# A selective scan on one core: the softplus through PSUM, all scaled tiles made by ScalarE, and its work placed at the head of a block

## The chip, the cores and the metric

The kernel runs on one NeuronCore of a Trainium2 chip, as one program in one launch. The metric is the time of an execution on the device, in microseconds. The engines are called as in the profile: PE is TensorE (PEld its weight loads), DVE is VectorE, ACT is ScalarE, POOL is GpSimd, SP is the queue that issues DMAs.

## The reference, cut to what matters

Eight samples of 256 channels on 32 x 32 positions go through four layers. The first three (attention with a gated feed-forward layer, a second attention, a quantised bottleneck) end in 8-bit codes in DRAM. The fourth is a state-space layer run in four directions over the 1024 positions, and all of the change but some prices lies there:

```python
def step(h, inp):
    u_t, dt_t, B_t, C_t = inp
    dA = jnp.exp(dt_t[:, :, None] * A)                      # A: 512 channels x 16 states
    h = h * dA + dt_t[:, :, None] * B_t[:, None, :] * u_t[:, :, None]
    y = jnp.einsum('bdn,bn->bd', h, C_t)
    return (h, y)
...
x = jax.nn.silu(xc).swapaxes(1, 2)
x_dbl = x @ W_x.T
dt = jax.nn.softplus(x_dbl[..., :DT_RANK] @ W_dt.T + b_dt)
...
y = _selective_scan(x, dt, A, Bm, Cm) + x * D
y = y * jax.nn.silu(z)
return y @ W_out.T
```

The four outputs (rows and columns, each forward and backward) are put back in place and added.

## The kernel before

The kernel has two phases. `phase_a` takes all samples through the first three layers; `phase_b` does the fourth.

Both are written as strands, Python generators that yield one operation or a list of them. `_Order.run` merges the strands into one program: it keeps its own clock for every engine, prices each operation in `_Op.__init__`, and always emits the operation that can start first by those clocks; at equal times the lower rank goes first. Each engine then executes its instructions in the order in which they were emitted, so the prices set the order of every queue but not the times on the chip. All operations are emitted in line 134, so the profile's groups are told apart by their tiles. Tiles come from rooms (`_Room`), each with a fixed number of buffers, and a strand that finds none waits.

In `phase_a` there is one thing more: where the order sees a gap on PE, `fill` puts in matmuls of constants (line 1077) that compute nothing needed, one for each 0.3 us of the gap.

`phase_b` works on blocks: 8 samples x 4 directions x 2 halves of 512 positions, 64 blocks, so that eight blocks make one sample. In a block there are 16 groups, one for each state s, and in each group four chunks c of 128 channels. The parts of a group are:

- `scales`: ACT multiplies duT (dt times x, positions on partitions; 128 x 512 for each of four position tiles t) with the column B of this state. The result is a tile of the room `dbu` (10 buffers). In every second group the last of the four position tiles is made another way: POOL multiplies the identity by B into a diagonal `dg`.
- `turns`: PE brings the four tiles of a chunk into a PSUM bank `db` (3 buffers) with channels on partitions. A scaled tile is transposed; for a diagonal, a full FP32 matmul of duT with the diagonal does the scaling and the turn at once.
- `decays`: ACT makes exp(dt * A) into `da` (5 buffers).
- `scans`: DVE runs the recurrence over 512 positions, from `da` and `db` into `h` (6 pairs). It frees `da` and `db`.
- `products`: POOL multiplies a pair of h by C, which a DMA spreads over the partitions (`cb`).
- `sums`: PE transposes the products and adds them up in four PSUM banks `py`.

Beside the groups there are jobs for blocks to come, started by `ahead` when the scans reach a given group: `mixed(n + 2)` (the convolution, the silu, B and C), `inputs` and `outputs` now and then, and `steps(n + 1)`, whose four dt jobs (one for each chunk) compute the softplus and duT, and entered at groups 0, 2, 4 and 6. These jobs rank ahead of all group work. They share one PSUM bank `pp`, taken with `lend()`.

A dt job computes the softplus as max(p, 0) + e - ((1 + e) - 1) + ln(1 + e), with e = exp(-|p|): ACT's Abs, Exp and Ln, DVE's `scalar_tensor_tensor` and `tensor_scalar`, and two POOL `tensor_tensor`. DVE then multiplies by x (tmp<-dt,xs), PE transposes the product (pp<-ident,tmp), and DVE copies it to duT (du<-pp).

Of the kernel before, what the change touches and what calls it, by code (L numbers as in the profile page):

```python
# [20 lines left out]
F32 = mybir.dt.float32  # L21
# [3 lines left out]
ALU = mybir.AluOpType  # L25
# [72 lines left out]
class _Op:  # L98


    def __init__(self, engine, method, args, kw):
        self.engine, self.method, self.args, self.kw = engine, method, args, kw
        out, ins = args[0], [a for a in (*args[1:], *kw.values()) if isinstance(a, bass.AP)]
        self.reads = {k for a in ins for k in self.blocks(a)}
        self.writes = {k for a in (out, kw.get("accum_out")) if a is not None for k in self.blocks(a)}
        self.landing = 0.0
        n = max(math.prod(a.shape[1:]) for a in (out, *ins)) / 1024
        near = all(a.space == out.space and out.space != PSUM for a in ins)
        if engine == "tensor":
            x = kw.get("rhs", ins[0])  # L110
            n = math.prod(x.shape[1:]) / 1024
            move = method == "transpose" or kw.get("is_transpose", False)
            self.cost = max(0.06, n * (0.93 if move else 0.44 if x.dtype != F32 else 1.76 if n > 0.2 else 2.1))
        elif engine == "vector":
            fast = near and method in ("tensor_scalar", "tensor_copy")
            both = near and method == "tensor_tensor"
            scan = method == "tensor_tensor_scan"
            self.cost = 0.04 + n * (2.2 if scan else 0.57 if fast else 1.1) + (0.3 if fast or both else 0)
        elif engine == "scalar":
            self.cost = 0.05 + 0.87 * n + (0.1 if len(ins) > 1 else 0)  # L120
        elif engine == "gpsimd":
            self.cost = 0.13 + 2.17 * n if method == "tensor_tensor" else 0.3 + n
        else:
            self.cost, self.landing = 0.1, 3.0

# [28 lines left out]
class _Room:  # L154
# [12 lines left out]
    def put(self, t):  # L167
        self.left.append(self.of.pop(t.name))


class _Order:
# [7 lines left out]
    def __init__(self, nc):  # L179
        self.nc, self.strands, self.n = nc, [], 0  # L180
        self.free, self.written, self.read, self.base, self.last = {}, {}, {}, {}, {}
        self.fill = None

    def add(self, rank, strand):
        self.n += 1
# [4 lines left out]
    def go(self, s, value=None):  # L190
        try:
            r = s[1].send(value)
            if isinstance(r, _Op):
                r = (r.cost, [r])
            elif isinstance(r, list):
                r = (sum(o.cost for o in r), r)
            s[2] = r
        except StopIteration:
            self.strands.remove(s)
# [63 lines left out]
def phase_a(ctx, tc, i, col, ident, codes, w_parts):  # L263
# [268 lines left out]
    def maxima(rank, q, k, rows, done):  # L532
# [6 lines left out]
        def some():  # L539
            while todo:  # L540
                yield lambda: not todo or may(2)
                if not todo:
                    break
                n = 4 if may(4) and not todo[0][2] else 2
                t, j, h = todo.pop(0)
                if n == 4 and todo:
                    todo.pop(0)
                bb = yield from some_banks(n)
                ops = []
                for e in range(n):  # L550
                    r = slice(32 * (h + e), 32 * (h + e) + 32)
                    ops.append(
                        T.matmul(bb[e], lhsT=q[r, t * P : (t + 1) * P], rhs=k[r, hs(j)], start=True, stop=True)
                    )
                yield (0.9 if n == 2 else 1.0, ops)
                for e in range(n):
                    m, s = (x[:, j, t, h + e : h + e + 1] for x in (least, sums))
                    yield V.tensor_reduce(m, bb[e], AX.X, ALU.max, negate=True)
                    yield A.activation(bb[e], bb[e], AF.Exp, bias=m, accum_out=s)
                    back(bb[e])  # L560
            left[0] -= 1
# [37 lines left out]
    def exponentials(rank, tasks, vt, n, finish):  # L599
# [5 lines left out]
        for task, (h, steps) in enumerate(tasks):  # L605
# [31 lines left out]
            def values(k, four, tiles, po=po, seen=seen, last=len(steps) - 1):  # L637
                es = [t[:, e] for t in tiles for e in range(2)]
                yield lambda: seen[0] == k
                ops = []  # L640
                for e, (q, kk, rows, key, r, c, at) in zip(es, four):
                    ops.append(
                        T.matmul(
                            po[at : at + n], lhsT=vt[:, key, c : c + n], rhs=e,
                            start=(k == 0 and key == 0), stop=(k == last), skip_group_check=True,
                        )
                    )
                yield (0.9 * (4 * n // P), ops)
                for t in tiles:
                    put(exps, t)  # L650
                seen[0] += 1
# [403 lines left out]
    def fill(gap, ops):  # L1055
# [6 lines left out]
            [order.last.get((bank.tag, k), 0.0) for k in bank.left] + [order.base.get(o.args[0].name, 0.0)] * own,  # L1062
            default=1e9,
        )
        n = int((gap - max(free, since)) / FILL)
        if n < 1:
            return
        if spare is not None and order.last.get((bank.tag, spare), 0.0) <= since:
# [9 lines left out]
        if t is not None:  # L1078
            bank.put(t)

    order.fill = fill
    stage = [0] * B

    def sample(b):
# [53 lines left out]
def phase_b(ctx, tc, i, col, ident, codes, w_parts, out):  # L1138
# [15 lines left out]
    xs_room = _Room(rooms, "xs", 11, [P, HALF])  # L1154
    dt_room = _Room(rooms, "dt", 2 * DC, [P, HALF])
    du_room = _Room(rooms, "du", 2, [P, TH, DI])
    db_room = _Room(rooms, "dbu", 10, [P, DI])
    dg_room = _Room(rooms, "dg", 4, [P, P])
    da_room = _Room(rooms, "da", 5, [P, HALF])
    h_room = _Room(rooms, "h", 6, [P, 2, HALF])  # L1160
    cb_room = _Room(rooms, "cb", 3, [P, HALF])
    tmp_room = _Room(rooms, "tmp", 3, [P, HALF])
    z_room = _Room(rooms, "z", 2, [P, HALF])
    cd_room = _Room(rooms, "cdb", 1, [P, CC, N], U8)
    wi_room = _Room(rooms, "wi", 2, [P, CC, 3, P], BF16)
# [29 lines left out]
    xds = [wp.tile([NX + 1, HALF], F32, name=f"xd{k}", tag=f"xd{k}") for k in range(2)]  # L1195
    for t in xds:
        nc.gpsimd.memset(t[2 * DS :], 1.0)
    zero = wp.tile([P, 1], F32, name="zero", tag="zero")
    nc.gpsimd.memset(zero, 0.0)
    yT = wp.tile([P, NT, DI], F32, name="yT", tag="yT")  # L1200
    ys = [wp.tile([P, N], F32, name=f"ys{c}", tag=f"ys{c}") for c in range(DC)]
    ctx.enter_context(tc.manual_schedule())
# [122 lines left out]
    def steps(n):  # L1325
# [6 lines left out]
        def dt(c):  # L1332
# [1 line left out]
            if c == 0:  # L1334
                d.duT[h] = yield from take(du_room)
            o = yield from take(dt_room)
            t, u1 = yield from takes(2, tmp_room)
            room, ps = yield from lend()
            yield T.matmul(ps, lhsT=w_dt[2 * DS :, c * P : (c + 1) * P], rhs=xd[2 * DS :], start=True, stop=True)
            left[0] -= 1  # L1340
# [4 lines left out]
            yield A.activation(t, ps, AF.Abs)  # L1345
            yield A.activation(t, t, AF.Exp, scale=-1.0)
            yield V.scalar_tensor_tensor(o, ps, 0.0, t, ALU.max, ALU.add)
            put(room, ps)
            yield V.tensor_scalar(u1, t, 1.0, -1.0, ALU.add, ALU.add)
            yield A.activation(t, t, AF.Ln, bias=1.0)  # L1350
            yield G.tensor_tensor(o, o, u1, ALU.subtract)
            yield G.tensor_tensor(o, o, t, ALU.add)
            put(tmp_room, t)
            d.dt[c, h] = o
            yield V.tensor_tensor(u1, o, d.xs[c, h], ALU.mult)
            yield lambda: h in d.duT
            room, pt = yield from lend()
            yield [T.transpose(pt[:, t * P : (t + 1) * P], u1[:, t * P : (t + 1) * P], ident) for t in range(TH)]
            put(tmp_room, u1)
            yield V.tensor_copy(d.duT[h][:, :, c * P : (c + 1) * P], pt.rearrange("p (t k) -> p t k", t=TH))  # L1360
            put(room, pt)
            done.add(("du", c))
# [76 lines left out]
    dbu, db, da, hh, cbs = {}, {}, {}, {}, {}  # L1439
    place = [0]  # L1440

    def scales(pick):


        for g, (n, d, h, s) in enumerate(groups):
            yield lambda: {("du", c) for c in range(DC)} | {"bT"} <= d.done[h]
            for t in range(TH):
                src, b = d.duT[h][:, t], d.bT[:, h * TH + t, s : s + 1]
                diagonal = t == TH - 1 and g % 2 == 0
                if diagonal != pick:  # L1450
                    continue
                if diagonal:
                    o = yield from take(dg_room)
                    yield G.tensor_scalar(o, ident, b, zero, ALU.mult, ALU.add)
                    dbu[g, t] = src, o
                else:
                    o = yield from take(db_room)
                    yield A.activation(o, src, AF.Identity, scale=b)
                    dbu[g, t] = o, ident

    def turns():
        for g, (n, d, h, s) in enumerate(groups):
            for c in range(DC):
# [1 line left out]
                ps = yield from take(ps_room)  # L1465
                yield [
                    T.matmul(
                        ps[:, t * P : (t + 1) * P], lhsT=dbu[g, t][0][:, c * P : (c + 1) * P], rhs=dbu[g, t][1],
                        is_transpose=dbu[g, t][1] is ident, start=True, stop=True,
                    )  # L1470
                    for t in range(TH)
                ]
                db[g, c] = ps
            for t in range(TH):
                o = dbu.pop((g, t))
                if o[1] is ident:
                    put(db_room, o[0])
                else:
                    put(dg_room, o[1])
            if s == DS - 1:  # L1480
                put(du_room, d.duT[h])

# [111 lines left out]
    def ahead():  # L1594

        for n in range(len(blocks)):
            jobs = []
            if n + 1 < len(blocks):
                jobs += zip((0, 2, 4, 6), steps(n + 1))
            if n + 2 < len(blocks):  # L1600
                jobs += zip((1, 3, 5, 7, 9, 10), mixed(n + 2))
            if n % 4 == 1 and n + 3 < len(blocks):
# [20 lines left out]
    for f in (list(inputs(0, False, xis[0, False])), mixed(0), steps(0), [behind(mixed(1))]):  # L1623
        for j in f:
            order.add((0, -1), j)
    for rank, f in enumerate((scans, decays, turns, lambda: scales(False), lambda: scales(True), products, sums, rows, ahead)):
        order.add((1, rank), f())
    order.add((0, -2), ends())
    order.run()
# [118 lines left out]
```

## Time and profile before

| | |
|---|---|
| median of three runs | 10703.6 us (10692.3 to 10710.2) |
| the profiled execution | 10710.8 us, span 10708.9 us |
| PE, DVE, ACT, POOL busy, share of the span | 92%, 79%, 81%, 63% |
| mean granted PE clock | 0.96 |
| 0 to 3747 us (to the first scan): PE, DVE, ACT, POOL busy | 3535, 2246, 2655, 911 us; clock 0.92 |
| 3747 to 10709 us: PE, DVE, ACT, POOL busy | 6364, 6241, 6047, 5826 us; clock 0.98 |

The profile is of one execution. The second phase repeats itself once per sample, which lets a view of one stretch stand for the others. Busy time of an instruction runs from its start to its end; instructions on PE and ACT overlap with those after them, so the distance between two starts in a row is shorter than a duration.

### The profile page before, as it was taken

The numbers are of one execution on the slowest core, as the hardware profiler recorded it, in microseconds if no ns is written. First come the engines' busy times: TensorE is split into PE (matmuls) and PEld (weight loads), VectorE is DVE, ScalarE is ACT, GpSimd is POOL, SyncE is SP. The second block draws the span as 40 slices with busy tenths as digits, with TensorE's granted clock in tenths as the row PEclk, the third lists the DMA queues.
The fourth block names the chain that finished last, engine by engine and source line by source line (L and its number), as shares of the span: only waits on it lengthen the run. The fifth ranks groups of instructions, "written<-read, shape, count | busy, mean of one in ns | idle before, by whom it ended". The sixth has DMA issues, their size and how long they took to land. (4 is left out here: it accounts for less than half of the span.)

```text
span 10708.9 us, 157325 instructions
## 1 busy us (share of the span) xinstructions
PE 9899.2 (92%) x58614; PEld 6251.0 (58%) x58726; DVE 8487.3 (79%) x8991; ACT 8702.0 (81%) x16284; POOL 6736.6 (63%) x3746
## 2 busy tenths in 40 slices
PE   9999999999999899899999999999989999998998
PEld 3333323333333267777777777777777777777776
DVE  5456657577675389888998998998899899899898
ACT  7867676777767488888888988888888888888988
POOL 1532133132220178888888888888888888888888
PEclk8998998999989899999999999999999999999999
DMA  1100000000000011111111111111111111111111
GB/s 53 32 18 16 22 17 22 13 22 13 14 13 10 20 46 41 48 52 47 47 46 52 50 42 56 41 49 52 45 48 52 47 47 46 51 50 43 56 40 50
DMA packets 217346, 410.01 MB, mean 38 GB/s; under 512 B 24881, under 2 KB 69297, under 8 KB 211458
## 3 DMA queue, kind: packets, MB, share of 16 engines
q1 hardware_dynamic: 216578, 399.94, 12.5%
q8 instruction: 461, 7.55, 0.3%
q14 instruction: 307, 2.51, 0.1%
HBM read 358.43 MB, written 30.93 MB: 36 GB/s over the span
## 5 line engine op out<-in xcount | busy, mean ns | idle before, releaser
L134 POOL TENSOR_TENSOR h<-h,cb 128x1024 f32<-128x1024 f32 x2048 | 4874.1, 2394 | 917.3 <-ACT st L134 462.7
L134 ACT ACTIVATE da<-dt,am 128x512 f32<-128x512 f32 x4096 | 2884.7, 717 | 515.6 <-DVE h L134 509.3
L134 DVE TENSOR_TENSOR_SCAN h<-da,st,db 128x512 f32<-128x512 f32 x2048 | 2469.2, 1260 | 177.2 <-PE db L134 96.9
L134 DVE TENSOR_TENSOR_SCAN h<-da,db 128x512 f32<-128x512 f32 x2048 | 2346.4, 1199 | 240.4 <-PE db L134 158.7
L134 ACT ACTIVATE dbu<-du,bT 128x512 f32<-128x512 f32 x3584 | 2487.7, 714 | 30.5 <-PE db L134 28.1
L134 PE MATMUL db<-ident,dbu 128*128 128x128 f32 x14336 | 2218.5, 280 | 169.1 <-DVE h L134 139.6
L134 PE MATMUL py<-ident,h 128*128 128x128 f32 x16384 | 2122.2, 275 | 91.5 <-POOL h L134 83.6
L134 PEld LDWEIGHTS db<-ident,dbu 128*128 128x128 f32 x14336 | 1669.9, 143 | 704.9 <-DVE h L134 377.9
L134 PEld LDWEIGHTS py<-ident,h 128*128 128x128 f32 x16384 | 1843.7, 142 | 168.4 <-POOL h L134 134.0
L134 DVE TENSOR_REDUCE stats<-bank 128x1 f32<-128x512 f32 x1536 | 983.0, 684 | 742.8 <-PE bank L134 741.3
L134 ACT ACTIVATE bank<-bank,stats 128x512 f32<-128x512 f32 x1536 | 1024.5, 672 | 380.9 <-DVE stats L134 370.4
L134 POOL TENSOR_TENSOR mid<-mid,mid 128x961 f32<-128x961 f32 (+2 forms) x192 | 400.3, 2092 | 1056.2 <-ACT mid L134 714.9
L134 PE MATMUL bank<-big,big 32*128 32x512 f32 x4096 | 913.3, 674 | 38.0 <-ACT bank L134 18.7
L134 PE MATMUL pp<-xi,cvd 128*128 128x512 f32 x2016 | 930.6, 605 | 3.5 <-DVE dt L134 1.5
L134 ACT ACTIVATE exps<-bank 128x512 f32<-128x512 f32 x1536 | 797.5, 620 | 135.6 <-PE bank L134 131.2
L134 PE MATMUL db<-dg,du 128*128 128x128 f32 x4096 | 809.0, 280 | 0.0
L134 DVE TENSOR_TENSOR tmp<-dt,xs 128x512 f32<-128x512 f32 x256 | 599.3, 2341 | 173.3 <-POOL dt L134 172.6
L134 POOL TENSOR_TENSOR dt<-dt,tmp 128x512 f32<-128x512 f32 x512 | 653.1, 1276 | 122.6 <-DVE tmp L134 97.5
L134 PEld LDWEIGHTS db<-dg,du 128*128 128x128 f32 x4096 | 636.2, 196 | 0.0
L134 DVE SCALAR_TENSOR_TENSOR mid<-mid,cols,mid 128x961 f32<-128x961 f32 (+1 forms) x384 | 597.2, 1555 | 6.9
L134 PEld LDWEIGHTS pp<-xi,cvd 128*128 128x128 f32 x2016 | 371.9, 195 | 384.3 <-issue 374.2
L134 PEld LDWEIGHTS bank<-big,big 32*128 32x128 f32 x4096 | 285.5, 193 | 503.2 <-issue 253.9
(212 smaller groups left out, 11329.5 us busy)
## 6 DMA issues: line engine op xcount, KB each, us to landing
cb<-c_d SPq DMA_DIRECT2D x1024, 256.0 KB, 3.2
wi<-w_in SPq DMA_DIRECT2D x192, 192.0 KB, 3.5
big<-in_x_dram SPq DMA_DIRECT2D x16, 1024.0 KB, 5.4
kept<-big SPq DMA_DIRECT2D x16, 1024.0 KB, 4.0
big<-kept SPq DMA_DIRECT2D x16, 1024.0 KB, 4.8
cdb<-codes SPq DMA_DIRECT2D x48, 256.0 KB, 4.2
big<-big SPq DMA_DIRECT2D x16, 512.0 KB, 6.7
out_dram<-z SPq DMA_DIRECT2D x32, 256.0 KB, 2.7
```

The source lines that it names most:

```text
L134: return getattr(getattr(nc, self.engine), self.method)(*self.args, **self.kw)
```

## The change

The edit has these parts:

- The softplus keeps its PSUM bank longer: (1 + e) - 1 is written over the bank instead of into a second SBUF tile, and DVE instead of POOL subtracts it. POOL instead of DVE multiplies dt by x, in place into the one tile t. The room `tmp` has 2 buffers, not 3, and a dt job takes one, not two.
- All four position tiles of every group are scaled by ACT and transposed; the diagonals, their room and their column of zeros are gone. The room `dbu` has 12 buffers, not 10.
- The dt jobs enter at groups 0, 1, 2 and 3.
- The ranks are reordered: decays and scales, which are ACT's, come after turns, products and sums.
- Prices of the order: matmuls over fewer than 20 rows cost 0.22 more, an ACT operation with a column operand 0.03 more, POOL's `tensor_tensor` 0.04 more. In `phase_a`, lists of PE operations get 0.1 more, three prices written by hand are set anew, and `fill` keeps 0.35 us of each gap.

```diff
-            self.cost = max(0.06, n * (0.93 if move else 0.44 if x.dtype != F32 else 1.76 if n > 0.2 else 2.1))
+            self.cost = max(0.06, (0.22 if x.shape[0] < 20 else 0) + n * (0.93 if move else 0.44 if x.dtype != F32 else 1.76 if n > 0.2 else 2.1))
...
-            self.cost = 0.05 + 0.87 * n + (0.1 if len(ins) > 1 else 0)
+            self.cost = 0.05 + 0.87 * n + (0.13 if len(ins) > 1 else 0)
         elif engine == "gpsimd":
-            self.cost = 0.13 + 2.17 * n if method == "tensor_tensor" else 0.3 + n
+            self.cost = 0.17 + 2.17 * n if method == "tensor_tensor" else 0.3 + n
...
-                r = (sum(o.cost for o in r), r)
+                r = (sum(o.cost for o in r) + self.way * (r[0].engine == "tensor"), r)
...
-                yield (0.9 if n == 2 else 1.0, ops)
+                yield (1.06, ops)
...
-                yield (0.9 * (4 * n // P), ops)
+                yield (0.88 * (4 * n // P) + 0.12, ops)
...
-        n = int((gap - max(free, since)) / FILL)
+        n = int((gap - max(free, since) - 0.35) / FILL)
...
-    order.fill = fill
+    order.fill, order.way = fill, 0.1
...
-    db_room = _Room(rooms, "dbu", 10, [P, DI])
-    dg_room = _Room(rooms, "dg", 4, [P, P])
+    db_room = _Room(rooms, "dbu", 12, [P, DI])
...
-    tmp_room = _Room(rooms, "tmp", 3, [P, HALF])
+    tmp_room = _Room(rooms, "tmp", 2, [P, HALF])
...
-            t, u1 = yield from takes(2, tmp_room)
+            t = yield from take(tmp_room)
...
             yield V.scalar_tensor_tensor(o, ps, 0.0, t, ALU.max, ALU.add)
+            yield V.tensor_scalar(ps, t, 1.0, -1.0, ALU.add, ALU.add)
+            yield A.activation(t, t, AF.Ln, bias=1.0)
+            yield V.tensor_tensor(o, o, ps, ALU.subtract)
             put(room, ps)
-            yield V.tensor_scalar(u1, t, 1.0, -1.0, ALU.add, ALU.add)
-            yield A.activation(t, t, AF.Ln, bias=1.0)
-            yield G.tensor_tensor(o, o, u1, ALU.subtract)
             yield G.tensor_tensor(o, o, t, ALU.add)
-            put(tmp_room, t)
             d.dt[c, h] = o
-            yield V.tensor_tensor(u1, o, d.xs[c, h], ALU.mult)
+            yield G.tensor_tensor(t, o, d.xs[c, h], ALU.mult)
...
-                diagonal = t == TH - 1 and g % 2 == 0
-                if diagonal != pick:
-                    continue
-                if diagonal:
-                    o = yield from take(dg_room)
-                    yield G.tensor_scalar(o, ident, b, zero, ALU.mult, ALU.add)
-                    dbu[g, t] = src, o
-                else:
-                    o = yield from take(db_room)
-                    yield A.activation(o, src, AF.Identity, scale=b)
-                    dbu[g, t] = o, ident
+                o = yield from take(db_room)
+                yield A.activation(o, src, AF.Identity, scale=b)
+                dbu[g, t] = o
...
-                        ps[:, t * P : (t + 1) * P], lhsT=dbu[g, t][0][:, c * P : (c + 1) * P], rhs=dbu[g, t][1],
-                        is_transpose=dbu[g, t][1] is ident, start=True, stop=True,
+                        ps[:, t * P : (t + 1) * P], lhsT=dbu[g, t][:, c * P : (c + 1) * P], rhs=ident,
+                        is_transpose=True, start=True, stop=True,
...
-                jobs += zip((0, 2, 4, 6), steps(n + 1))
+                jobs += zip((0, 1, 2, 3), steps(n + 1))
...
-    for rank, f in enumerate((scans, decays, turns, lambda: scales(False), lambda: scales(True), products, sums, rows, ahead)):
+    for rank, f in enumerate((scans, turns, products, sums, decays, scales, rows, ahead)):
```

More of the change, by code (lines that the diff above doesn't have):

```diff
@@ L181, in __init__ @@
         self.free, self.written, self.read, self.base, self.last = {}, {}, {}, {}, {}
-        self.fill = None
+        self.fill, self.way = None, 0.0
     def add(self, rank, strand):
@@ L1197, in phase_b @@
         nc.gpsimd.memset(t[2 * DS :], 1.0)
-    zero = wp.tile([P, 1], F32, name="zero", tag="zero")
-    nc.gpsimd.memset(zero, 0.0)
     yT = wp.tile([P, NT, DI], F32, name="yT", tag="yT")
@@ L1347, in dt @@
             yield V.scalar_tensor_tensor(o, ps, 0.0, t, ALU.max, ALU.add)
+            yield V.tensor_scalar(ps, t, 1.0, -1.0, ALU.add, ALU.add)
+            yield A.activation(t, t, AF.Ln, bias=1.0)
+            yield V.tensor_tensor(o, o, ps, ALU.subtract)
             put(room, ps)
-            yield V.tensor_scalar(u1, t, 1.0, -1.0, ALU.add, ALU.add)
-            yield A.activation(t, t, AF.Ln, bias=1.0)
-            yield G.tensor_tensor(o, o, u1, ALU.subtract)
             yield G.tensor_tensor(o, o, t, ALU.add)
-            put(tmp_room, t)
             d.dt[c, h] = o
-            yield V.tensor_tensor(u1, o, d.xs[c, h], ALU.mult)
+            yield G.tensor_tensor(t, o, d.xs[c, h], ALU.mult)
             yield lambda: h in d.duT
             room, pt = yield from lend()
-            yield [T.transpose(pt[:, t * P : (t + 1) * P], u1[:, t * P : (t + 1) * P], ident) for t in range(TH)]
-            put(tmp_room, u1)
+            yield [T.transpose(pt[:, k * P : (k + 1) * P], t[:, k * P : (k + 1) * P], ident) for k in range(TH)]
+            put(tmp_room, t)
             yield V.tensor_copy(d.duT[h][:, :, c * P : (c + 1) * P], pt.rearrange("p (t k) -> p t k", t=TH))
@@ L1440, in phase_b, with scales @@
     place = [0]
-    def scales(pick):
+    def scales():
         for g, (n, d, h, s) in enumerate(groups):
@@ L1474, in turns @@
             for t in range(TH):
[L1475 to L1479, printed above, removed]
+                put(db_room, dbu.pop((g, t)))
             if s == DS - 1:
```

## The prediction

> **What bounds the kernel now.** I read the busy time by stretches first. The scans start at 3747 us and fill the rest of the span; from 4077 us on the kernel repeats itself once per sample (eight blocks), so I cut the span at seven samples.
>
> ```profile
> core 0: us, PE busy (x) PEld busy (x) DVE busy (x) ACT busy (x) POOL busy (x), PEclk, DMA share, GB/s
> 6691.70:7563.30 871.60, 799.22 (x5379) 623.80 (x5394) 783.43 (x714) 759.31 (x1322) 729.57 (x409) 0.98 0.17 48
> ...
> sum 6094.00, PE 5587.71 PEld 4363.68 DVE 5480.19 ACT 5312.78 POOL 5108.57; mean PE 798.24 PEld 623.38 DVE 782.88 ACT 758.97 POOL 729.80
> ```
>
> A sample takes 6094/7 = 870.6 us, in which PE is busy 798, DVE 783, ACT 759, POOL 730. Nothing is saturated: four engines lie within 8% of each other, each with 70 to 140 us of waiting. So the second question is what they wait for (the waits of all engines from 4000 to 10500 us, 6500 us, or 7.47 samples):
>
> ```profile
> ACT da L134 <- DVE h L134: 480.8, 451, 5.7
> PE pp L134 <- DVE tmp L134: 188.2, 141, 2.1
> DVE tmp L134 <- POOL dt L134: 166.3, 106, 3.0
> ACT st L134 <- DVE h L134: 136.7, 172, 2.5
> ACT tmp L134 <- DVE tmp L134: 65.2, 86, 1.5
> ```
>
> Columns are us in total, times, longest. ACT's main wait is for one of the five da tiles, which a DVE scan frees: DVE is late. PE and DVE also wait for each other around tmp, the softplus. The third view is the groups with shapes kept apart, same window:
>
> ```profile
> L134 POOL TENSOR_TENSOR h<-h,cb 128x1024 f32<-128x1024 f32 x1918 | 4566.2, 2394 | 866.3 <-ACT st L134 428.7 <-DVE h L134 260.1 <-issue 53.5
> L134 ACT ACTIVATE da<-dt,am 128x512 f32<-128x512 f32 x3835 | 2700.4, 717 | 483.9 <-DVE h L134 480.8
> L134 ACT ACTIVATE dbu<-du,bT 128x512 f32<-128x512 f32 x3355 | 2328.6, 714 | 29.1 <-PE db L134 27.9
> ...
> L134 PE MATMUL db<-dg,du 128*128 128x128 f32 x3836 | 758.2, 280 | 0.0
> ...
> L134 DVE TENSOR_TENSOR tmp<-dt,xs 128x512 f32<-128x512 f32 x239 | 569.2, 2382 | 167.1 <-POOL dt L134 166.3
> ...
> L134 DVE TENSOR_SCALAR tmp<-tmp 128x512 f32<-128x512 f32 x239 | 271.2, 1135 | 0.0
> ...
> L134 POOL TENSOR_SCALAR dg<-ident,bT,zero 128x128 f32<-128x128 f32 x479 | 243.6, 509 | 69.8 <-PE db L134 69.0
> ```
>
> Two DVE steps cost more than their size: a 512-column multiply takes 2382 ns. The view of the tile tmp (min/median/max) shows why that is not its own work:
>
> ```profile
> L134 DVE TENSOR_SCALAR tmp<-tmp x239: 409/694/2589, 4004.1 to 10486.5; 128x512 f32<-128x512 f32 x120
> L134 DVE TENSOR_TENSOR tmp<-dt,xs x239: 666/2601/2852, 4009.8 to 10490.4; 128x512 f32<-128x512 f32 x120
> ```
>
> Alone the multiply takes 666 ns; mostly it takes two microseconds more, about one POOL h product (2394 ns).
>
> **What the skill says.** "SBUF — State Buffer", section "Who interferes with whom": a DVE instruction with two SBUF inputs, or in a two-port mode such as tensor_scalar from SBUF to SBUF, contends with GpSimd for a shared port, and the loser blocks for the whole instruction; with at most one SBUF input outside those modes it doesn't. The two rows agree. "TensorE: Matmul & The Clock Gate", section "Terms", calls transpose mode 4x faster for FP32; here it is 2x: in the PE instructions in order of time a diagonal product is two passes 0.11 us apart, a transpose one such pass. "ScalarE: Activation LUTs", section "What ACT_TABLE_LOAD costs", says that back-to-back ACTIVATEs overlap by about 93 ns; starts of dbu in a row lie 614 ns apart against 714 ns long, so I price them at 0.614 us.
>
> **The change, per sample** (32 dt jobs, 128 groups).
> - **DVE.** The multiply leaves: 32 x 2.38 = -76. tensor_scalar now writes PSUM, out of the two-port mode: 1.135 becomes about 0.67, the row of dt<-pp,tmp (667 ns): -15. The subtract comes in with one PSUM input; the three DVE steps now run in a row, starts 0.58 apart: +19. DVE 783 - 72 = 711. Bound: the contention stays with the tensor_scalar (2.5 us at most, +45) or all costs fall to 0.58 (-5); I take the table row.
> - **POOL.** 64 diagonals at 0.509 leave: -33. The subtract (1.275) is exchanged for the multiply, same shape and engine: 0. POOL 730 - 33 = 697.
> - **PE.** 64 x 4 diagonal products lose one pass: 256 x 0.11 = -28. The transposes of the softplus waited 188.2/7.47 = 25 us for the DVE multiply; now they wait for POOL. If a product comes in between, that is 32 x 2.34 = 75 us; if POOL's two steps follow at once, nothing. The order's own price of a POOL tensor_tensor (0.17 + 2.17/2 = 1.26 us) fits the measured 1.275, whereas it gave the DVE multiply 0.89 against 2.38, so PE's queue was placed 1.5 us too early; I take 10. Behind that wait stand turns and sums. PE 770.
> - **ACT.** 64 scaled tiles come in: 64 x 0.614 = +39. ACT 759 + 39 = **798**, now the busiest, at just what PE has today.
> - **Lent bank.** A dt job holds pp, the one spare PSUM bank, 4.2 us today (first matmul to the end of scalar_tensor_tensor); two more DVE steps make it 5.4: 32 x 1.2 = +38 us of pp. Folds, convs and projections queue behind it, with deadlines of a block or more. Taken as nothing; at worst +38.
> - **Order.** dt jobs enter at groups 0 to 3 of a block, not 0, 2, 4, 6. In those four groups POOL has 8 x 2.33 + 8 x 1.23 = 28.5 us and ACT some 28, against 27 of a quarter block: a lag of under 2 us, within the h tiles (three groups) and the twelve dbu. The results are needed a block later. The ranks keep decays before scales on ACT and turns before sums on PE, so they only break ties: 0. DMAs and the SP queue are unchanged.
>
> **From work to time.** ACT's period is its busy time plus its idle time, now 870.6 - 759 = 112. By the waits (divided by 7.47): da 64, st 18, tmp<-tmp 9, pp results 12, dbu 4, rest 5. The da wait arises when DVE frees no da tile, above all in a dt job: 0.67 + 1.135 + 2.38 + 0.70 of waiting = 4.9 us each, 156 per sample; after, some 1.8 us, 58. In proportion 64 becomes 24, and as ACT gets 39 us slower against DVE I take 12. st 13, tmp 6, pp results 12, rest 3: **46**. Period 798 + 46 = 844, -26 per sample, x 8 = **-210 us**.
>
> **The first phase** (to 3747 us) has the same code but other prices in its order: higher PE costs and 0.35 us kept back in every gap before filler matmuls are put in.
>
> ```profile
> L1077 PE MATMUL bank<-minus x1622: 376/379/634, 1.6 to 3657.7; 128*128 128x512 bf16 x175, 128*64 128x512 bf16 x6
> ```
>
> Counting in PE's order of time, the 1622 fillers stand in 445 runs, starts 0.215 us apart; after 359 of the runs the next matmul starts at once, so the run may have made it late. One filler less per run is 445 x 0.215 = 96 us of PE queue; I count **-40**, as DVE is only 60% and ACT 71% busy here and the chain is often theirs. Bounds: -110, and +60 if a lower clock (0.92 here) or the new order costs more.
>
> Sum against the profiled execution (span 10708.9, 10710.8 us in all, 7 above the median 10703.6): 10710.8 - 250 = 10461, or 10455 on the scale of the median.
>
> **Rivals.**
> 1. *ACT closes up (slower).* The scaled tiles go to what becomes the busiest engine and its waits stay, because the bunched dt jobs in the first four groups still stop scans and da tiles. Break-even is an ACT idle of 870.6 - 798 = 72 per sample (without the first phase). At 85 it costs 13 x 8 = 102, less 40: 10710.8 + 62 - 7 = 10766. For it: in before no engine passes 92%, and ACT would have to run at 94.6%. Against: 64 of its 112 idle us hang on a DVE that loses 72. Chance 0.13.
> 2. *Half of it (small or no gain).* The transposes wait for POOL (75) or the pp bank (38) eats what DVE gives: idle 65, -7 x 8 - 20 = -76, 10628. Chance 0.12, a third of it within the noise.
> 3. *More.* With prices that fit, ACT hardly stalls (idle 22, 97%): 820, -50 x 8 - 60 = -460, 10244. DVE scans do run back to back in quiet groups now. Chance 0.13.
>
> The forecast has 0.62, by itself from 10320 to 10630. The range over all cases is 10250 to 10720. A measurement of this kernel can tell 0.2% (21 us) from no change: faster 0.62 + 0.13 + 0.08 = 0.83, same 0.04, slower 0.13.
>
> **What would show it.** A sample near 844 us with ACT about 798 busy and above PE; DVE about 711, POOL about 697; no tmp<-dt,xs on DVE and no DVE row of the softplus over 0.7 us; da<-DVE h falling from 481 to some 90 in a like window; PE's wait for tmp now on POOL and under 75; fewer than 1250 fillers. It would be wrong if ACT's idle stayed over 72 per sample, if PE stayed the busiest, or if the first phase moved by more than 100.

## The result, and the profile after

The changed kernel takes 10311.6 us (median of four runs, 10309.9 to 10314.2) against 10706.9 for the kernel before, measured again beside it: a ratio of 0.9635, 95% interval 0.962 to 0.9651. The forecast was 10455 in a range of 10250 to 10720: right in sign, inside the range, but 143 us too slow. The profiled execution took 10309.9 us (span 10308.2), 401 less than the one before.

The first view is again the busy time by stretches, cut at the first scan and at seven samples.

```profile
core 0: us, PE busy (x) PEld busy (x) DVE busy (x) ACT busy (x) POOL busy (x), PEclk, DMA share, GB/s
0.00:3698.40 3698.40, 3447.14 (x15022) 1295.69 (x15023) 2255.81 (x3326) 2643.96 (x5756) 889.73 (x491) 0.90 0.06 21
3698.40:10308.20 6609.80, 6152.72 (x40960) 4742.00 (x40958) 5724.99 (x5671) 6304.93 (x11035) 5523.44 (x2736) 0.97 0.17 50
```

```profile
6478.40:7304.80 826.40, 771.68 (x5137) 593.75 (x5136) 717.68 (x714) 791.03 (x1385) 691.91 (x345) 0.97 0.17 51
...
sum 5779.50, PE 5407.34 PEld 4162.84 DVE 5022.64 ACT 5539.83 POOL 4842.20; mean PE 772.48 PEld 594.69 DVE 717.52 ACT 791.40 POOL 691.74
```

Of the 401 us, 49 lie in the first phase and 352 in the second. A sample takes 5779.5/7 = 825.6 us, not 870.6. ACT has become the busiest, at 791, and it now stands still for only 34 us of a sample, where it stood still for 112. The waits of ACT, over these seven samples (5779.5 us; in total, times, longest), show which of its stops went:

```profile
ACT da L134 <- DVE h L134: 154.5, 279, 1.9
ACT st L134 <- DVE h L134: 25.7, 69, 0.4
ACT xs L134 <- PE pp L134: 12.9, 42, 1.0
ACT tmp L134 <- PE pp L134: 12.9, 25, 1.1
ACT dbu L134 <- PE db L134: 10.4, 25, 1.4
ACT tmp L134 <- DVE pp L134: 2.3, 7, 0.3
```

The view of the tile tmp and of pp (min/median/max) shows the softplus on its new engines. No DVE row is stretched any more; compare 409/694/2589 and 666/2601/2852 before.

```profile
L134 DVE TENSOR_SCALAR pp<-tmp x238: 694/695/697, 4006.2 to 10096.7; 128x512 f32<-128x512 f32 x119
...
L134 POOL TENSOR_TENSOR tmp<-dt,xs x237: 1264/1277/1292, 4010.6 to 10092.8; 128x512 f32<-128x512 f32 x119
```

```profile
L134 DVE TENSOR_TENSOR dt<-dt,pp x238: 659/661/667, 4008.0 to 10098.4; 128x512 f32<-128x512 f32 x119
```

DVE's own idle time has grown, from 88 us to 108 per sample: in this window its scans wait 467.5 us for db, the bank that PE fills. That does not make it free time, as e_multdve below shows.

### The profile page after: what moved, and what is told of

Its sections match the earlier page's. It is cut to its first block, busy times and chain, and to the rows that moved or that the text cites. A ratio compares the mean times of both kernels' runs of the same rounds, so it can differ in the third digit from the quotient of the medians.

```text
span 10308.2 us, 152318 instructions
## 1 busy us (share of the span) xinstructions
PE 9599.9 (93%) x55980; PEld 6037.7 (59%) x55980; DVE 7980.8 (77%) x8997; ACT 8948.9 (87%) x16790; POOL 6413.2 (62%) x3227
## 3 DMA queue, kind: packets, MB, share of 16 engines
q1 hardware_dynamic: 216578, 399.94, 12.9%
## 4 chain that ended last, share of the span: by engine, by line
PE 38%; ACT 33%; DVE 21%; issue 5%; POOL 2%; DMA 1%; SPq 0%; DVEq 0%; POOLq 0%; ACTq 0%
PE bank L134 20%; ACT da L134 12%; ACT dbu L134 11%; DVE h L134 8%; PE pp L134 7%; PE py L134 5%; DVE mid L134 5%; PE db L134 5%; DVE stats L134 3%; ACT xs L134 2%; DVE dt L134 2%; ACT tmp L134 2%; PE bank L1077 1%; ACT z L134 1%; ACT bank L134 1%
## 5 line engine op out<-in xcount | busy, mean ns | idle before, releaser
L134 POOL TENSOR_TENSOR h<-h,cb 128x1024 f32<-128x1024 f32 x2048 | 4815.7, 2373 | 898.5 <-ACT st L134 322.4
L134 ACT ACTIVATE dbu<-du,bT 128x512 f32<-128x512 f32 x4096 | 2806.8, 709 | 12.5 <-PE db L134 10.6
L134 PE MATMUL db<-ident,dbu 128*128 128x128 f32 x16384 | 2411.4, 283 | 300.0 <-DVE h L134 208.2
L134 PEld LDWEIGHTS db<-ident,dbu 128*128 128x128 f32 x16384 | 1909.5, 144 | 870.4 <-DVE h L134 388.3
L134 PE MATMUL bank<-big,big 32*128 32x512 f32 x4096 | 958.9, 685 | 40.8 <-ACT bank L134 29.9
L134 PEld LDWEIGHTS bank<-big,big 32*128 32x128 f32 x4096 | 331.1, 197 | 523.9 <-issue 206.1
L134 POOL TENSOR_SCALAR big<-big,ga,gs 128x512 f32<-128x512 f32 x64 | 59.8, 948 | 818.6 <-DVE gs L134 480.5
L134 PE MATMUL bank<-exps,big 128*32 128x512 f32 (+1 forms) x3072 | 552.0, 627 | 3.7 <-ACT exps L134 3.7
L134 PE MATMUL bank<-big 32*128 32x512 f32 x2048 | 509.5, 724 | 21.3 <-ACT bank L134 17.9
L134 POOL TENSOR_TENSOR big<-big,mid 128x961 f32<-128x961 f32 (+1 forms) x128 | 315.1, 2470 | 227.0 <-ACT mid L134 224.4
```

What stands on the lines that cost most here:

```text
L134: return getattr(getattr(nc, self.engine), self.method)(*self.args, **self.kw)
```

## The experiments

I had two questions: which part carries the 352 us of the second phase, and why they were more than the 210 of the forecast. Each kernel was timed in three rounds against the kernel before. All samples below are blocks 3 to 58 of the profiled execution, divided by seven; ACT idle is the sample's time less ACT's busy time.

| kernel | time, us | ratio to before, 95% | first scan | sample | ACT busy | ACT idle |
|---|---|---|---|---|---|---|
| before | 10706.9 | | 3747 | 870.6 | 759 | 112 |
| after | 10311.6 | 0.9635 (0.962 to 0.9651) | 3698 | 825.6 | 791 | 34 |
| a_softplus | 10524.3 | 0.9827 (0.9811 to 0.9844) | 3745 | 848.5 | 758 | 91 |
| b_nodiag | 10718.8 | 1.0015 (1.0008 to 1.0022) | 3745 | 871.8 | 794 | 78 |
| c_first | 10659.3 | 0.9953 (0.9938 to 0.9968) | 3706 | 870.2 | 758 | 112 |
| h_place_alone | 10684.2 | 0.998 (0.9973 to 0.9987) | 3758 | 867.3 | 758 | 109 |
| f_price | 10822.0 | 1.0111 (1.0094 to 1.0128) | 3933 | 860.5 | 760 | 101 |
| e_multdve | 10543.1 | 0.9848 (0.9828 to 0.9868) | 3716 | 855.4 | 794 | 61 |
| k_diag | 10393.6 | 0.9713 (0.9695 to 0.9732) | 3692 | 836.9 | 757 | 80 |
| d_place | 10407.9 | 0.972 (0.9705 to 0.9734) | 3703 | 838.9 | 791 | 48 |
| m_apart | 10421.2 | 0.9732 (0.9717 to 0.9746) | 3708 | 839.7 | 794 | 46 |
| i_prices | 10394.1 | 0.9704 (0.9688 to 0.972) | 3717 | 836.1 | 793 | 43 |
| j_ranks | 10456.5 | 0.9766 (0.9743 to 0.9789) | 3702 | 843.3 | 793 | 51 |
| g_conv | 10294.2 | 0.9614 (0.9599 to 0.9628) | 3695 | 824.7 | 775 | 50 |

### One part alone, on the kernel before

**a_softplus.** The new softplus only:

```diff
-            t, u1 = yield from takes(2, tmp_room)
+            t = yield from take(tmp_room)
...
+            yield V.tensor_scalar(ps, t, 1.0, -1.0, ALU.add, ALU.add)
+            yield A.activation(t, t, AF.Ln, bias=1.0)
+            yield V.tensor_tensor(o, o, ps, ALU.subtract)
...
+            yield G.tensor_tensor(t, o, d.xs[c, h], ALU.mult)
```

> The kernel before with the softplus part alone: (1+e)-1 into the PSUM bank, the subtract on DVE, the multiply on POOL, two tmp tiles; diagonals, order of the dt jobs and all prices as before. Theory T (DVE's contention with POOL was what starved ACT of da tiles): most of the gain of the second phase is here, a sample falls from 871 to about 840 us, -240 us in all (ratio 0.978), the da<-DVE h wait halves at least. Rival D (what counts is PE's and POOL's relief from the diagonals): -60 us (0.994).

Measured: 183 us faster, all of it in the second phase (6776.7 us from the first scan on, before 6961.6). ACT's work is unchanged and its idle time falls by 21 us per sample. Its da wait falls from 447.3 us in seven samples to 254.1. So theory T is right on the direction and high on the size: 183, not 240, and the da wait falls by 43%, not by the half that it asked for. The run does not part two things: DVE loses no time to POOL any more, and the order's price of the multiply now fits (f_price takes up the second). Another wait grew in the same view:

```profile
ACT da L134 <- DVE h L134: 254.1, 377, 2.5
ACT xs L134 <- PE pp L134: 238.3, 114, 6.0
```

ACT's wait for the convs of pp was 59.3 and is 238.3. A dt job now holds the lent bank for 6.9 us in the kernel after (from its first matmul to the end of the subtract, mean of 252 jobs in the list of instructions) and 6.6 here, against 4.2 before.

**b_nodiag.** All tiles scaled by ACT, no diagonals:

```diff
-                diagonal = t == TH - 1 and g % 2 == 0
-                if diagonal != pick:
-                    continue
...
+                o = yield from take(db_room)
+                yield A.activation(o, src, AF.Identity, scale=b)
```

> The kernel before with all four tiles of a group scaled by ACT and transposed, no diagonals, eleven dbu tiles (twelve do not fit beside three tmp tiles); softplus, order and prices as before. Theory T: ACT gets 39 us of work per sample more, DVE stays late, so a sample goes from 871 to 875 or 890 us, +30 to +150 us (ratio 1.003 to 1.014). Rival D: PE and POOL lose 28 and 33 us per sample and that carries the gain: -200 us or more (0.981).

Measured: 11 us slower, just clear of zero. ACT's work grows by 35 us per sample and its idle time shrinks by 34. Rival D falls: with the old softplus, relief of PE and POOL is worth what it costs ACT and no more.

**c_first.** The first phase's edits alone, from `yield (1.06, ops)` to `order.fill, order.way = fill, 0.1` of the diff.

> The kernel before with the first phase's edits alone: the three prices written by hand, 0.1 us per list of PE operations, 0.35 us kept back in each gap before fillers. Both theories: the second phase stays within 5 us; the first falls by about 50 us (ratio 0.995), with some 950 fillers for 1622. If the change of the first phase came from the shared prices of operations instead, less than 15 us.

Measured: 48 us faster, the first scan 42 us earlier, a sample 870.2. Fewer fillers and the new prices came together here, so the run does not say which of the two paid. The fillers, in the view of line 1077:

```profile
L1077 PE MATMUL bank<-minus x946: 376/379/634, 1.6 to 3614.6; 128*128 128x512 bf16 x177, 128*64 128x512 bf16 x13
```

**h_place_alone.** `zip((0, 1, 2, 3), steps(n + 1))` in the kernel before.

> The kernel before with the dt jobs at groups 0, 1, 2, 3 and nothing else: here a dt job gives its pp bank back right after scalar_tensor_tensor. Theory B (the place pays because the softplus now holds the one lent bank longer, and convs no longer have to share the groups with it): little or nothing, within 30 us of before (ratio 0.997 to 1.003). Rival O (bunching at the head pays by itself): some 90 us faster (0.992 or less).

Measured: 21 us faster, as theory B had it, though its interval just excludes 1. In the profiled execution the second phase is 30 us shorter and the first, with the same instructions as before, 11 us longer: so much can a first scan differ by itself. The place was worth more at the other end of the change, as d_place shows.

**f_price.** Only what the order believes of DVE:

```diff
-            self.cost = 0.04 + n * (2.2 if scan else 0.57 if fast else 1.1) + (0.3 if fast or both else 0)
+            self.cost = 0.04 + n * (2.2 if scan else 0.57 if fast else 1.1) + (0.8 if fast else 1.8 if both else 0)
```

> The kernel before with one price changed: the order counts DVE's SBUF-to-SBUF tensor_tensor at 2.4 us and tensor_scalar at 1.1 us in the two phases, as measured; nothing else. Theory T: the time itself is lost on DVE and stays lost, so at most 40 us faster (ratio 0.996 or more). Rival P (the order was wrong because its price was wrong): PE no longer waits 25 us per sample for tmp, 100 us or more faster (0.990 or less).

Measured: 117 us slower, and neither theory meant that. The price also holds in the first phase, where the order then sees longer gaps and fills them: 2586 fillers for 1622, and the first scan comes 186 us later. The second phase went the other way, from 6961.6 to 6892.8, 69 us faster. So rival P has a share: some of what the multiply cost was that the order did not know its time. PE's wait for tmp did not vanish by it (PE pp <- DVE tmp is still 96.4 us in seven samples).

### One part taken back, from the kernel after

**e_multdve.** `yield V.tensor_tensor(t, o, d.xs[c, h], ALU.mult)` in place of POOL's.

> The kernel after with the multiply of dt by x put back on DVE (two SBUF inputs), at the order's old price of 0.89 us. Theory T (DVE's wait for POOL's port holds the scans and so the da tiles): the DVE row of the multiply is 2 us or more again, ACT's da wait grows from 154 to 300 us or more in a like window, 100 us or more slower than the kernel after (ratio to before 0.973 or more). Rival S (DVE has slack now, 108 us per sample idle): 66 us of contention per sample is absorbed, within 30 us of the kernel after (0.966 or less).

Measured: 232 us slower. Rival S falls, although DVE was idle for 108 us of a sample. The groups of DVE show a stretched multiply again, though at 1.6 us and not the 2 or more that T expected; min/median/max from the tile's view stand below it:

```profile
L134 DVE TENSOR_TENSOR tmp<-dt,xs 128x512 f32<-128x512 f32 x224 | 354.7, 1583 | 1.1 <-POOL dt L134 0.9
```

```profile
L134 DVE TENSOR_TENSOR tmp<-dt,xs x228: 665/1507/2837, 4044.0 to 10079.7; 128x512 f32<-128x512 f32 x114
```

The shortest is 665 ns, the mean 1583, which agrees with the shared port of the Trainium skill's page "SBUF — State Buffer", section "Who interferes with whom". DVE gets 32 x 1.58 = 51 us of work per sample, 29 of them contention; the sample grows by 30, ACT's idle time by 27. The da wait is 220.9, not the 300 that T expected; ACT's wait for st (103.9 for 25.7) and PE's for dbu (113.2 for 56.6) grew as well.

**k_diag.** The diagonals back in, with ten dbu tiles and four dg tiles.

> The kernel after with the diagonals back (every second group, one position tile of four; ten dbu tiles and four dg), the new softplus, order and prices kept. Theory T: ACT loses 32 us of work per sample and PE gets 28, POOL 33; PE becomes the busiest at some 800 and the sample takes 835 us, 80 us slower than the kernel after (ratio 0.971). Rival A (ACT is the bound, so taking work from it pays): 100 us faster than the kernel after (0.954).

Measured: 82 us slower, as theory T had it. With the new softplus the extra ACT work is worth having, with the old one (b_nodiag) it was not. PE is the busiest again, at 791 us of a sample to ACT's 757, and the da wait more than doubles:

```profile
ACT da L134 <- DVE h L134: 351.1, 493, 3.3
```

**d_place.** The dt jobs back at groups 0, 2, 4, 6.

> The kernel after with the dt jobs back at groups 0, 2, 4, 6. Theory T: no one waits for dt within the block, so within 0.3% of the kernel after (10280 to 10340 us, ratio to before 0.960 to 0.966). Rival O (the place in the block matters): slower than the kernel after by 100 us or more (ratio 0.973 or above).

Measured: 96 us slower, just short of the 100 of rival O and far from theory T: my prediction, which gave the order 0, is wrong on this. ACT's waits pointed to the lent bank:

```profile
ACT da L134 <- DVE h L134: 182.4, 258, 3.2
ACT xs L134 <- PE pp L134: 80.3, 98, 3.5
```

The xs wait was 12.9 in the kernel after. From that I made theory B: dt jobs that hold pp longer, alternating with convs that need it.

**m_apart.** Dt jobs at 0, 2, 4, 6, but mixed moved out of their way:

```diff
-                jobs += zip((0, 1, 2, 3), steps(n + 1))
+                jobs += zip((0, 2, 4, 6), steps(n + 1))
...
-                jobs += zip((1, 3, 5, 7, 9, 10), mixed(n + 2))
+                jobs += zip((8, 9, 10, 11, 12, 13), mixed(n + 2))
```

> The kernel after with the dt jobs back at groups 0, 2, 4, 6 (as in d_place, which was 96 us slower than the kernel after) and the jobs of mixed, convs first, moved from groups 1, 3, 5, 7, 9, 10 to 8 to 13, so that dt jobs and convs meet less at the one lent bank. Theory B (d_place lost its time where convs and dt jobs with a longer hold alternate on pp): ACT's wait of xs for PE pp falls back from 80 to 30 us or less and the loss is gone, 10300 to 10345 us (ratio 0.962 to 0.967). Rival O (dt results early in the block are what pays): still about 10410 (0.972).

Measured: 110 us slower, no better than d_place. The xs wait did fall by 43%, though not to 30, and the time did not follow; others took its place:

```profile
ACT da L134 <- DVE h L134: 171.9, 277, 2.8
ACT xs L134 <- PE pp L134: 46.1, 76, 1.3
ACT dbu L134 <- PE db L134: 38.8, 70, 1.9
```

So nothing here supports theory B as the explanation of d_place. It is not a clean refutation: the silu and the projection of mixed moved with the convs, which is a new disturbance of the order.

**i_prices.** The three shared prices as before (no 0.22 for few rows, 0.10 for a column operand, 0.13 for POOL).

> The kernel after with the three shared prices of the order as they were (no 0.22 for few rows, ACT's column operand 0.10, POOL's tensor_tensor 0.13 base). Theory T: a few hundredths of a us move no queue by much, within 30 us of the kernel after (ratio 0.961 to 0.967). Rival P (prices that fit carry what is left of the gain, about 80 us that the single parts do not add up to): 10390 (0.970).

Measured: 83 us slower. Theory T, which gave such small prices nothing, is wrong here too. Of the 95 us between the two profiled executions, 19 are a first scan that comes later (946 fillers for 924), and the sample has grown by 10.4.

**j_ranks.** By now three unlike disturbances had cost 83 to 110 us. I took the ranks for pure tie-breaks, and so took them back as a control:

```diff
-    for rank, f in enumerate((scans, turns, products, sums, decays, scales, rows, ahead)):
+    for rank, f in enumerate((scans, decays, turns, scales, products, sums, rows, ahead)):
```

> The kernel after with the ranks in the old order (decays, turns, scales, products, sums), which decide only between operations that could start at the same time; every price, place, buffer and instruction is that of the kernel after. Theory T (as predicted: ranks only break ties): within 30 us of the kernel after, 10285 to 10340 us (ratio 0.961 to 0.966). Rival C (the greedy order is so sensitive that any disturbance of the settled order costs about what d_place, i_prices and m_apart cost, 80 to 110 us, whatever it is): 10390 us or more (0.970).

Measured: 145 us slower, the most of all. The program has the same instructions in another order. In seven samples:

```profile
4015.20:9918.50 5903.30, 5471.27 (x35944) 4198.20 (x35941) 5027.63 (x4984) 5547.72 (x9691) 4843.32 (x2409) 0.97 0.17 50
```

DVE and POOL are as busy as in the kernel after (5022.64 and 4842.20), ACT by 8 us more and PE by 64 in 5900; what has grown is the stops: da 205.7 for 154.5, DVE's copy to du waiting for PE's pp 115.8 for 3.1, PE's db waiting for dbu 108.5 for 56.6. And there is one that the kernel after does not have at all, in the view of all waits of the same window:

```profile
PEld py L134 <- ACT yT L134: 39.6, 31, 3.5
...
PE py L134 <- ACT yT L134: 20.8, 12, 2.7
```

It says that the control was not one. By the order's clock an operation whose inputs are there can start when its engine is free, so everything that is ready and waits for a busy engine is tied, and there the rank is a priority. Within one engine the two lists differ in one thing: `sums`, which ends every second block with two copies of py by ACT (yT<-py), stands behind decays and scales in the old list and ahead of them in the new one. In this run these copies end a median of 18.1 us after the block's last product, in the kernel after 11.9; the py banks come free later, and PE's queue stands. The wait for yT lies in group 2 of the block that follows, and all but about 1 of the 115.8 us of du in groups 2 and 4 of the same blocks (counted from 0). Of the 124 us that this run loses in seven samples, 97 lie in 14 of the 56 blocks: in each four, the one behind the first of the two that end with such copies. That is read from one pair of traces; no run moves `sums` alone.

**g_conv.** ACT being the busiest, I moved the conv's bias to DVE:

```diff
-            yield A.activation(t, ps, AF.Identity, bias=col("cv_b", c))
+            yield V.tensor_scalar(t, ps, col("cv_b", c), None, ALU.add)
```

> The kernel after with the conv's bias added by DVE's tensor_scalar from PSUM instead of ACT: ACT loses 32 x 0.58 = 19 us of work per sample (791 to 772, the same as PE), DVE gets 32 x 0.65 = 21 (717 to 738). If ACT's work is the bound, the sample falls from 826 to about 810, 10190 us (ratio 0.952). If PE and ACT bind together by their queue order, no more than 40 us (0.960).

Measured: 10294.2 us, 17 below the kernel after, but the intervals (0.9599 to 0.9628 and 0.962 to 0.9651) overlap, so it isn't shown to beat it. ACT's work did fall by 16 us per sample, and its idle time grew by 15, above all by waiting for the dbu tiles that PE frees (81.8 us in seven samples for 10.4). That is what the second expectation meant: ACT's work alone does not bound the sample.

## Why the prediction was right or wrong

**DVE, POOL, PE, ACT: right.** Per sample, forecast and measured: DVE 711 and 717.5, POOL 697 and 691.7, PE 770 and 772.5, ACT 798 and 791.4. tensor_scalar into PSUM takes 695 ns, for 0.67 assumed. The 64 scaled tiles cost ACT 32 us instead of 39. About 2 of the 7 are more overlap (it grew by 8 us per sample, where 0.1 us for each tile makes 6); most of the rest is that ACT's instructions got a little shorter, da 713 ns for 717 and dbu 709 for 713, for which the runs show no reason. Three of the forecast's sums are slightly off, without weight for it: 13 x 8 is 104, not 102; 10461 less 7 is 10454; and the +45 for contention that stays is counted from 1.135 us, where from the 0.67 of the sum it would be 59.

**The cause: right in direction, and in part argued.** With the multiply on POOL and the tensor_scalar in PSUM, DVE frees da tiles sooner; a_softplus alone brings 183 us with no change of ACT's work, and e_multdve alone takes 232 back. How much of it is contention is not parted from the order's price of the multiply: the price alone brought the second phase 69 us in f_price. PE's wait for tmp is gone as forecast, but POOL, for which 10 us per sample were taken, hardly took its place (2.3 us in seven samples). For pp PE now waits until DVE's subtract frees the lent bank, 26.9 us in seven samples, a wait that the forecast had put at nothing.

**ACT's idle time: mis-sized, 34 for 46.** By term: da 22 (forecast 12), st 4 (13), tmp behind DVE 0.3 (6), pp results 4 (12), dbu and the rest 4 (3). The da wait was underrated, most of the others overrated, so that the sum came nearer than its terms was luck. Over the forecast's 7.47 samples the da wait would be 165 us, where I looked for some 90. Together with ACT's 7 us less of work this makes 825.6 for 844, 18 us per sample, and 352 for 210 in all: these two terms are nearly the whole of the miss.

**The step that failed is "Order: 0".** I argued that dt results are needed a block later and that the ranks only break ties, so neither could matter. d_place, i_prices and j_ranks each take back one edit of the order, and each costs 83 to 145 us; their ACT idle times are 48, 43 and 51, so the 34 of the kernel after needs all three. That the 46 which I had summed from the waits lies among these is not shown to be more than chance. The losses do not add: 96 + 83 + 145 is 324, of some 400 in all, of which the softplus has 183 for itself and the first phase 49. For the ranks the error can be named: I compared decays with scales and turns with sums, and overlooked the copies of py that `sums` puts on ACT. For the place and the prices the runs do not show why they pay; bank, convs and da tiles each explain a part of a wait and none the time. Nor does every change of the kernel after cost this much: g_conv lost nothing. Open as well is how much of the 82 us of k_diag, which also has ten dbu tiles for twelve, and of e_multdve's 232 is diagonals and multiply, and how much is the disturbed order.

**The lent bank** was taken as nothing and held for 5.4 us; it is held for 6.9. In a_softplus ACT's waits for the convs in pp are 179 us longer in seven samples than before. Whether that is why this kernel reached 848 and not 840 isn't shown: in m_apart a shorter wait of this kind brought no time.

**The first phase: right,** -49 for -40, with 924 fillers, and c_first gives 42 of it alone. The granted clock did fall, 0.92 to 0.90, without undoing the gain. f_price shows the other direction: 964 fillers more went with 186 us more.

**Rivals.** The slower one (ACT closes up) did not occur: ACT's idle time fell far below the 72 of break-even. But b_nodiag comes near to it: with the old softplus, 35 us more work on ACT bring 34 less idle time and 11 us more in all. The third rival, ACT at 97% and 10244 us, was nearer to the result (ACT runs at 95.9%) than its chance of 0.13 said.

## What to carry to other kernels

When several engines are within a tenth of each other, look first for an instruction whose spread (666 to 2852 ns) shows that it waits inside itself, and move it to where it waits for no one. Do not expect all of the freed time back: in a_softplus DVE lost 66 us of work per sample, and the sample fell by 22. Idle time on an engine is no proof that it can take work: in e_multdve DVE had 108 us idle per sample, got some 50 more of work, and the sample grew by 30. In this kernel, work given to the engine that became the busiest paid only once the engine it waited for was relieved (b_nodiag against k_diag). And in a program whose queues are ordered by a greedy planner, a part's worth can't be read from undoing it alone, since undoing it moves the order too. Before you call a rank a tie-break, list all that each strand puts on each engine: on a busy queue the rank is a priority.

## What the runs showed that I had not expected

The ranks alone moved this kernel by 145 us (1.4%) with the same instructions, more than the diagonals (82). And a price nearer to what the second phase shows made the kernel slower, by 117 us: the second phase gained 69, but the first, where the same prices decide on the fillers, lost 186 with 964 more of them.
